# Two chunks' head products in one group, the bias product on two row tiles, and longer planned gaps in a gated state-space and expert layer

## The chip, the cores and the metric

The kernel runs on one core of a Trainium2 chip. The metric is the device time of one execution in microseconds (us). A core has a matrix engine (PE, with its weight loads shown apart as PEld), a vector engine (DVE), an activation engine (ACT), a general engine (POOL) and a queue that starts transfers (SP). Each executes its own instructions in order and waits on semaphores for the others. SBUF is the on-chip memory of 128 partitions; PSUM is the memory of eight banks of 128 x 512 fp32 that PE writes its products into.

## What is computed

The input is x, 8 sequences of 2048 tokens of 256 numbers. A modulation row per sequence gives shifts, scales and gates. The layer has two halves.

```
h = layernorm(x) * (1 + ca) + sa
x = x + ga * mamba(h)          # W_in, causal convolution, state space scan, gate by silu(z), RMS norm, W_out
h = layernorm(x) * (1 + cb) + sb
x = x + gb * experts(h)        # softmax gate over 8 experts, those under 0.1 dropped, sum of weight * (h @ W_e + b_e)
```

The scan is done by chunks. With C, B, the steps dt and the running sum cs of dt * A within a chunk, one of 8 heads of 64 channels gives

```
y[i] = sum over j <= i of (C_i . B_j) exp(cs_i - cs_j) dt_j x_j  +  exp(cs_i) C_i . state  +  D x_i
state' = exp(cs_last) state + sum over j of exp(cs_last - cs_j) dt_j B_j x_j
```

and y * silu(z) is squared and summed over 512 channels for the RMS norm. The reference uses chunks of 64 tokens; the kernel computes the same scan in chunks of 128.

## The kernel before, in words

The work is cut into 32 blocks of 512 tokens (8 sequences, 4 blocks each), and a block into four chunks of 128 tokens. Everything is fp32; a matrix product is issued by PE as two instructions, so the counts of the profile are twice those of the program. Weights stay in SBUF.

The steps of a block are generators. A planner (`run`) holds a heap of generators with due times; it takes the earliest, lets it write its next instructions, and puts it back later by what it yields. One planned block is `PERIOD` = 70. `STARTS` gives each step's first due time within its block, so that some four blocks are open at once: `fetch` (-20), `first_norm` (-9), `project_xbc` (11.5), `project_z` (42), `silu_xbc` (47.5), `output` (128), `gate_weights` (151) and `experts` (186); `within` starts for chunk c at 54 + 17.5 c. The planned clock decides only the order in which instructions are written, and with it the order on each engine of the built program; no engine waits for it.

PSUM is handed out by the planner too. `take(use)` gives the bank that has been free longest, at most `MOST[use]` to one use ("ex" expert products, "pj" projections, "y" heads, "m" the rest). `give` says that a bank is free again `READ_TIME` = 3.0 after the reader was written. The true protection is a semaphore: a product into a reused bank waits for the last reader.

The steps that the change touches:

- `spread` (L508) loads, for one chunk, the running sums cs of the 8 heads to all 128 partitions, into the first half of the tile `wide` (128 x 2 x 8 x 128).
- `within` (L517) makes the second half from it by eight Relu instructions on ACT (L526), then four transposes of x on PE (L536), that of B (L537) and the product B by C (L539); one Exp over both halves on ACT (L540); on DVE the scaled x, `xdt` (L543), the masked product (L547), B (L549) and the weights of the 8 heads, in place in `wide` (L561); on POOL `xdec` (L556) and `cw` (L564). Then come the products of the heads (L579): 8 of `xdt` by the weights and 8 of `state` by `cw`, each 64 columns wide, two heads side by side in the array; the state product (L587) with its decay on POOL (L590); on DVE the skip term (L600, four instructions), the gate by silu(z) (L603) and the new state (L609, or L607 at a start); at last the squares on ACT (L616) and their sums on POOL (L618, L619), into `sqs`.
- `output` (L626) transposes `sqs` (L633), which turns the squares by channel into rows by token, reduces them, and multiplies by W_out (L646); `residual` (L655) adds to x.
- `gate_weights` makes the second norm and the gate: a product (L673), a copy (L679), its transpose (L681), a softmax on DVE and ACT (L696), and the transposed weights `wtt` (L712, L715). `eb_sb` holds the experts' biases: rows 32 c to 32 c + 7 of column block c.
- `experts` (L739) starts `res` with the product of `wtt` and `eb_sb` (L748, two products of 128 x 512 with all 128 rows of the array, most of which are zeros) and an ACT copy (L753). Then follow 16 pairs of expert products (L759), each read by two DVE instructions (L722); POOL adds to x and SP stores the block.

Of the kernel before, what the change touches and what calls it, by code (L numbers as in the profile page):

```python
# [11 lines left out]
AF = mybir.ActivationFunctionType  # L12
# [3 lines left out]
P = 128  # L16
# [9 lines left out]
def kernel(  # L26
# [51 lines left out]
    const = ctx.enter_context(tc.tile_pool(name="const", bufs=1))  # L78
    psum = ctx.enter_context(tc.tile_pool(name="psum", bufs=1, space=bass.MemoryType.PSUM))
    N_BANKS = 8  # L80
    MOST = {"ex": 3, "pj": 2, "y": 1, "m": 4}


    ident = new(const, [P, P], "ident")
# [5 lines left out]
    neg_half = new(const, [P, NC], "neg_half")  # L90
    nc.gpsimd.memset(neg_half, -0.5)

    io = ctx.enter_context(tc.tile_pool(name="io", bufs=4))

    pb = ctx.enter_context(tc.tile_pool(name="per_batch", bufs=2))
    blk = ctx.enter_context(tc.tile_pool(name="block", bufs=2))
# [411 lines left out]
    def spread(n, c):  # L508

        yield from until(info[n], "cs_d")  # L510
        wide = info[n]["wide", c] = new(chk, [P, 2, NH, P], "wide")
        nc.sync.dma_start(
            out=wide[:, 0], in_=info[n]["cs_d"][c * QD : c * QD + NH, :].partition_broadcast(P)
        )
        yield

    def within(n, c):  # L517


        d = info[n]  # L520
        yield from until(d, "tok", ("wide", c))
        xbc, tok_major, wide = d["xbc"], d["tok"], d["wide", c]
        tok = ts(c, P)
        bt, ct_ = xbc[:, MB, tok], xbc[:, MCC, tok]
        for h in range(NH):
            nc.scalar.activation(  # L526
                wide[:, 1, h, :], wide[:, 0, h, :], AF.Relu, bias=tok_major[:, 1, c, h : h + 1]
            )
# [11 lines left out]
        nc.scalar.activation(wide, wide, AF.Exp, scale=-1.0)  # L540
        yield 1.2
        xdt = new(chk, [P, DI], "xdt")
# [17 lines left out]
        up_to, w = wide[:, 0], wide[:, 1]  # L560
        nc.vector.tensor_tensor(w, w, sm[:, None, :].to_broadcast([P, NH, P]), ALU.mult)  # L561
        yield 1.8
        cw = new(chk, [P, NH, P], "cw")
        nc.gpsimd.tensor_tensor(cw, up_to, ct_[:, None, :].to_broadcast([P, NH, P]), ALU.mult)  # L564
        yield 2.0
        if c > 0:
            yield from until(d, ("state", c - 1))
        elif s_of(n) > 0:
            yield from until(info[n - 1], ("state", NC - 1))
        yield 3.5  # L570
        state = carry.get("state") if (s_of(n), c) != (0, 0) else None


        y_ps = yield from take("y")
        parts = [(xdt, w)] if state is None else [(xdt, w), (state, cw)]
        for i, (lhs, rhs) in enumerate(parts):
            for h in range(NH):
                m, q = divmod(h, 2)
                nc.tensor.matmul(  # L579
                    y_ps[ts(q, HEADDIM), ts(m, P)], lhs[:, ts(h, HEADDIM)], rhs[:, h, :],  # L580
                    start=(i == 0 and m == 0), stop=(i == len(parts) - 1),
                    skip_group_check=True,
                )
        if not last:

            st_ps = yield from take("m")
            nc.tensor.matmul(st_ps[:, :DI], bm, xdec, start=True, stop=True)  # L587
            behind = new(blk, [P, DI], "state", bufs=3)
            if state is not None:
                nc.gpsimd.tensor_tensor(  # L590
                    by_head(behind), by_head(state), per_head(up_to[:, :, P - 1]), ALU.mult
                )
            carry["state"] = behind
        d["state", c] = True
        yield from until(d, *(("z_silu", m) for m in range(MI)))
        yield 1.4
        y = y_ps.rearrange("p (m t) -> p m t", m=MI)
        g = d["zs"]
        for m in range(MI):
            nc.vector.scalar_tensor_tensor(  # L600
                y[:, m, :], xbc[:, m, tok], d_ch[:, m : m + 1], y[:, m, :], ALU.mult, ALU.add
            )
        nc.vector.tensor_tensor(g[:, :, tok], y, g[:, :, tok], ALU.mult)  # L603
        give(y_ps)
# [6 lines left out]
        yield 1.8  # L611

        if c == 0:
            d["sqs"] = new(sml, [P, NC, P], "sqs", bufs=1)
        sq = new(chk, [P, MI, P], "sq", bufs=1)
        nc.scalar.activation(sq, g[:, :, tok], AF.Square)  # L616
        yield 0.8
        nc.gpsimd.tensor_add(sq[:, 0:2, :], sq[:, 0:2, :], sq[:, 2:4, :])  # L618
        nc.gpsimd.tensor_add(d["sqs"][:, c, :], sq[:, 0, :], sq[:, 1, :])  # L619
        d["y", c] = True  # L620

    def s_of(n):
        return order[n][1]
# [2 lines left out]
    def output(n):  # L626
        b, s = order[n]
        d = info[n]
        yield from until(d, *(("y", c) for c in range(NC)))
        wo = gated[b][0]  # L630
        s_ps = yield from take("m")
        for c in range(NC):
            nc.tensor.transpose(s_ps[:, ts(c, P)], d["sqs"][:, c, :], ident)  # L633
        yield 1.2
        ms = new(sml, [P, NC], "ms")
        nc.vector.tensor_reduce(ms, s_ps.rearrange("p (c t) -> p c t", c=NC), AX.X, ALU.add)
        give(s_ps)
        yield 0.9
        rs = new(sml, [P, NC], "rs")
        inv_sqrt(rs, ms, 1.0 / DI)  # L640
        yield 1.0
        d["mv"] = new(sml, [P, NC, 2], "mv1")
        for c in range(NC):
            o_ps = yield from take("m")
            for m in range(MI):
                nc.tensor.matmul(  # L646
                    o_ps[:, :DM], d["zs"][:, m, ts(c, P)], wo[:, m, :],
                    start=(m == 0), stop=(m == MI - 1),
                )
            after(2.2, residual(n, c, o_ps, rs))  # L650
            yield OUT_STEP
# [11 lines left out]
    def gate_weights(n):  # L663
# [13 lines left out]
        yield 1.2  # L677
        head = new(sml, [P, P], "head", bufs=1)
        nc.scalar.copy(head, lg_ps[:, :P])  # L679
        yield 1.5  # L680
        nc.tensor.transpose(lg_ps[:, P : 2 * P], head, ident)  # L681
        yield 1.0

# [22 lines left out]
        nc.vector.scalar_tensor_tensor(wsum, wsum, 0.0, wsum, ALU.is_equal, ALU.add)  # L706
        nc.vector.reciprocal(wsum, wsum)
        nc.vector.tensor_mul(w, w, over(wsum))
        yield 6.5

        wt_ps = yield from take("m")
        nc.tensor.transpose(wt_ps[:, :P], wt.rearrange("p c q -> p (c q)"), ident)  # L712
# [26 lines left out]
    def experts(n):  # L739
        d = info[n]  # L740
        yield from until(d, "wtt")
        ht, wtt = d["ht", 1], d["wtt"]
        per = 512 // DM

        res = new(blk, [P, NC, DM], "res")
        for c in range(0, NC, per):
            b_ps = yield from take("m")
            nc.tensor.matmul(  # L748
                b_ps, wtt, eb_sb[:, c : c + per, :].rearrange("p c o -> p (c o)"),
                start=True, stop=True,  # L750
            )
            yield 1.2
            nc.scalar.copy(res[:, c : c + per, :].rearrange("p c o -> p (c o)"), b_ps)  # L753
            give(b_ps)
        for c in range(NC):
            for e in range(0, NE, per):
                ps = yield from take("ex")
                for k in range(KD):
                    nc.tensor.matmul(  # L759
                        ps, ht[:, k, ts(c, P)],  # L760
                        we_sb[:, k, e : e + per, :].rearrange("p e o -> p (e o)"),
                        start=(k == 0), stop=(k == KD - 1),
                    )
# [58 lines left out]
```

## Time and profile before

| what | value |
| --- | --- |
| median of 3 runs | 2448.13 us (2447.92 to 2448.78) |
| the profiled execution, its own time | 2448.43 us |
| span of its profile | 2446.6 us |
| mean granted PE clock | 0.992 |
| busy DVE / ACT / POOL | 1850.2 / 1437.3 / 1094.1 us |
| instructions | 33352 |

The profile describes one execution. Busy time of an engine is the time in which it executes anything. The timeline gives start, duration, engine, line, operation and output<-inputs, with equal neighbours merged; since matrix products overlap at their ends, the distance from start to start tells what one costs. The table of waits says which instruction stood idle and what released it.

### The profile page before, as it was taken

The page shows a single profiled execution, that of the slowest core. Times are in us where ns is not written, and L with a number is a line of the kernel's source. Part 1 is how long each engine was busy: PE and PEld are TensorE (multiplying, and loading weights), DVE is VectorE, ACT ScalarE, POOL GpSimd, SP SyncE. Part 2 cuts the span into 40 slices and gives each one's busy share as a digit, 9 for nine tenths or more (in the row PEclk, how much of TensorE's full clock was granted, in tenths as well). Part 3 has the DMA queues.
Part 4 walks back from the last instruction along what each step waited for, and adds up shares of the span by engine and source line. Part 5 has one row for each costly group of instructions (what it writes and reads, how often), then busy time and mean ns, then how long its engine had stood idle before and what let it go on. Part 6 is the DMA issues. An engine that isn't in the chain of part 4 may idle for free.

```text
span 2446.6 us, 33352 instructions
## 1 busy us (share of the span) xinstructions
PE 2356.1 (96%) x11474; PEld 1312.8 (54%) x11474; DVE 1850.2 (76%) x4414; ACT 1437.3 (59%) x2685; POOL 1094.1 (45%) x1244
## 2 busy tenths in 40 slices
PE   7899999999999999999999999999999999999998
PEld 3555555555555555555555555555555555555554
DVE  5677877777777777877777877878777777778775
ACT  6776666566566556655665565665556656555630
POOL 3544444444444434444444444444445444454441
PEclk8899999999999999999999999999999999999999
DMA  5111111111111111011111011110111111111100
GB/s 153 37 36 45 41 40 45 53 45 45 39 42 45 52 45 45 31 49 45 44 46 53 28 45 48 49 45 28 50 46 45 45 37 44 45 44 54 36 27 18
DMA packets 64600, 110.49 MB, mean 45 GB/s; under 512 B 7048, under 2 KB 47024, under 8 KB 64432
## 3 DMA queue, kind: packets, MB, share of 16 engines
q1 hardware_dynamic: 64416, 108.35, 13.2%
q8 instruction: 92, 1.51, 0.3%
q14 instruction: 76, 0.62, 0.1%
q10 hardware_dynamic: 16, 0.01, 0.0%
HBM read 89.47 MB, written 18.87 MB: 44 GB/s over the span
## 4 chain that ended last, share of the span: by engine, by line
PE 37%; DVE 21%; ACT 20%; POOL 11%; DMA 7%; issue 3%; SPq 0%; ACTq 0%; POOLq 0%; DVEq 0%
PE bank L759 15%; DVE xbc L372 6%; PE bank L409 5%; PE bank L445 5%; POOL cw L564 5%; ACT wide L526 5%; ACT wide L540 5%; DMA wide<-cs_d 4%; PE bank L579 4%; DVE res L722 3%; ACT xn L328 3%; DVE bank L600 2%; PE bank L646 2%; DMA xt<-_attn_hidden_states_dram 2%; POOL rstd L311 2%
## 5 line engine op out<-in xcount | busy, mean ns | idle before, releaser
L759 PE MATMUL bank<-we_sb,ht 128*128 128x512 f32 x2048 | 976.3, 599 | 41.4 <-DVE zs L603 39.2
L759 PEld LDWEIGHTS bank<-we_sb,ht 128*128 128x128 f32 x2048 | 368.7, 191 | 390.6 <-issue 367.2
L722 DVE SCALAR_TENSOR_TENSOR res<-bank,wt,res 128x256 f32<-128x256 f32 x1024 | 485.3, 474 | 99.8 <-PE bank L759 65.6
L372 DVE SCALAR_TENSOR_TENSOR xbc<-bank,conv_w_sb,xbc 128x509 f32<-128x509 f32 (+2 forms) x576 | 426.3, 742 | 82.0 <-ACT halo L368 78.2
L526 ACT ACTIVATE wide<-wide,tok_major 128x128 f32<-128x128 f32 x1024 | 329.0, 388 | 199.4 <-DMA wide<-cs_d 141.1
L564 POOL TENSOR_TENSOR cw<-wide,xbc 128x1024 f32<-128x1024 f32 x128 | 315.6, 2466 | 186.4 <-ACT wide L540 133.9
L409 PE MATMUL bank<-ht,w_in_sb 128*128 128x512 f32 x768 | 365.3, 598 | 3.0 <-ACT ht L340 2.6
L590 POOL TENSOR_TENSOR state<-state,wide 128x512 f32<-128x512 f32 x112 | 118.6, 1059 | 285.4 <-DVE state L609 263.4
L540 ACT ACTIVATE wide<-wide 128x2048 f32<-128x2048 f32 x128 | 244.7, 1912 | 2.3
L328 ACT ACTIVATE xn<-xt,shift,rstd 128x256 f32<-128x256 f32 x256 | 135.4, 591 | 182.8 <-DVE shift L324 182.8
L646 PE MATMUL bank<-wo,zs 128*128 128x256 f32 x1024 | 242.7, 380 | 0.0
L600 DVE SCALAR_TENSOR_TENSOR bank<-xbc,d_ch,bank 128x128 f32<-128x128 f32 x512 | 179.5, 351 | 82.3 <-PE bank L579 75.6
L445 PE MATMUL bank<-ht,w_in_sb 128*128 128x512 f32 x512 | 240.9, 594 | 0.0
L618 POOL TENSOR_TENSOR sq<-sq 128x256 f32<-128x256 f32 x128 | 103.1, 805 | 287.0 <-ACT sq L616 282.8
L409 PEld LDWEIGHTS bank<-ht,w_in_sb 128*128 128x128 f32 x768 | 141.0, 192 | 160.7 <-issue 131.6
L646 PEld LDWEIGHTS bank<-wo,zs 128*128 128x128 f32 x1024 | 192.2, 190 | 64.8 <-issue 33.7
L730 POOL TENSOR_TENSOR res<-res,gates 128x256 f32<-128x256 f32 x128 | 93.5, 731 | 258.0 <-DVE res L722 258.0
L561 DVE TENSOR_TENSOR wide<-wide,sm 128x1024 f32<-128x1024 f32 x128 | 204.2, 1595 | 0.0
L556 POOL TENSOR_TENSOR xdec<-xdt,tok_major 128x512 f32<-128x512 f32 x120 | 132.9, 1108 | 126.1 <-DVE xdt L543 120.3
L364 ACT ACTIVATE xbc<-bank,conv_b_sb,conv_w_sb 128x512 f32<-128x512 f32 x192 | 147.2, 767 | 35.8 <-PE bank L409 35.6
L616 ACT ACTIVATE sq<-zs 128x512 f32<-128x512 f32 x128 | 79.8, 624 | 147.3 <-DVE zs L603 94.2
L445 PEld LDWEIGHTS bank<-ht,w_in_sb 128*128 128x128 f32 x512 | 96.3, 190 | 119.2 <-issue 106.5
(127 smaller groups left out, 3098.8 us busy)
## 6 DMA issues: line engine op xcount, KB each, us to landing
wide<-cs_d SPq DMA_DIRECT2D x128, 512.0 KB
xt<-_attn_hidden_states_dram SPq DMA_DIRECT2D x32, 512.0 KB
out_dram<-xt SPq DMA_DIRECT2D x32, 512.0 KB
we_sb<-in_L_ffn_expert_w_dram SPq DMA_DIRECT2D x8, 256.0 KB
cs_d<-cs SPq DMA_DIRECT2D x32, 64.0 KB
ht<-in_L_wmod_dram SPq DMA_DIRECT2D x2, 512.0 KB
w_in_sb<-in_L_attn_W_in_dram SPq DMA_DIRECT2D x1, 776.0 KB
w_in_sb<-in_L_attn_W_in_dram SPq DMA_DIRECT2D x1, 512.0 KB
```

Of the source, the lines that this page charges most:

```text
L328: nc.scalar.activation(xn[:, c, :], src[:, c, :], AF.Identity, bias=shift[:, c : c + 1], scale=rstd[:, c : c + 1],)
L372: nc.vector.scalar_tensor_tensor(acc[:, ahead:], ps[:, : T - ahead], conv_w_sb[:, m, k : k + 1], acc[:, ahead:], ALU.mult, ALU.add,)
L409: nc.tensor.matmul(ps, w_in_sb[:, k, DI + m * P : DI + (m + 1) * P], ht[:, k, :], start=(k == 0), stop=(k == KD - 1),)
L445: nc.tensor.matmul(ps, w_in_sb[:, k, ts(m, P)], ht[:, k, :], start=(k == 0), stop=(k == KD - 1),)
L526: nc.scalar.activation(wide[:, 1, h, :], wide[:, 0, h, :], AF.Relu, bias=tok_major[:, 1, c, h : h + 1])
L540: nc.scalar.activation(wide, wide, AF.Exp, scale=-1.0)
L561: nc.vector.tensor_tensor(w, w, sm[:, None, :].to_broadcast([P, NH, P]), ALU.mult)
L564: nc.gpsimd.tensor_tensor(cw, up_to, ct_[:, None, :].to_broadcast([P, NH, P]), ALU.mult)
L600: nc.vector.scalar_tensor_tensor(y[:, m, :], xbc[:, m, tok], d_ch[:, m : m + 1], y[:, m, :], ALU.mult, ALU.add)
L646: nc.tensor.matmul(o_ps[:, :DM], d["zs"][:, m, ts(c, P)], wo[:, m, :], start=(m == 0), stop=(m == MI - 1),)
L722: nc.vector.scalar_tensor_tensor(res, ps[:, ts(q, DM)], wt[:, c, e + q : e + q + 1], res, ALU.mult, ALU.add)
L759: nc.tensor.matmul(ps, ht[:, k, ts(c, P)], we_sb[:, k, e : e + per, :].rearrange("p e o -> p (e o)"), start=(k == 0), stop=(k == KD - 1),)
```

## The change

Heads. `wide` keeps only cs and its exponential; the weights get a tile `w` of their own with three buffers, `xdt` and `cw` get three and the state four. The one Exp over 2048 elements becomes two over 1024. `within` now writes the state product (now L576), its decay (L579) and the new state (L590) and stores the operands of the heads. After the second and the fourth chunk a new function, `outputs`, takes two banks and writes the head products of two chunks as one run of 32 (L608), then for each of the two the skip term (L620), the gate (L624), the squares (L631) and the sums (L633, L634).

Biases. The two products over 128 rows become four products of 64 rows and 256 columns (L768), in turns on the upper and the lower rows, into two banks that are taken together; the two copies (L774) follow.

Planned times. `READ_TIME` goes from 3.0 to 4.5, the yield before the gate's transpose (now L697) from 1.5 to 3.5, that before the transposed weights (L728) from 6.5 to 8.0; `output` yields 5.0 before the transposed squares (L649); `gate_weights` starts at 156 and `experts` at 198; the input tiles get five buffers, not four, and "y" two banks. The expert products are now L781 and their readers L738.

```diff
-    MOST = {"ex": 3, "pj": 2, "y": 1, "m": 4}
+    MOST = {"ex": 3, "pj": 2, "y": 2, "m": 4}
-    io = ctx.enter_context(tc.tile_pool(name="io", bufs=4))
+    io = ctx.enter_context(tc.tile_pool(name="io", bufs=5))
 def spread(n, c):
-        wide = info[n]["wide", c] = new(chk, [P, 2, NH, P], "wide")
+        wide = info[n]["wide", c] = new(chk, [P, NH, P], "wide")
 def within(n, c):
+        w = new(chk, [P, NH, P], "w", bufs=3)
         for h in range(NH):
             nc.scalar.activation(
-                wide[:, 1, h, :], wide[:, 0, h, :], AF.Relu, bias=tok_major[:, 1, c, h : h + 1]
+                w[:, h, :], wide[:, h, :], AF.Relu, bias=tok_major[:, 1, c, h : h + 1]
             )
...
         nc.scalar.activation(wide, wide, AF.Exp, scale=-1.0)
+        nc.scalar.activation(w, w, AF.Exp, scale=-1.0)
...
-        y_ps = yield from take("y")
-        parts = [(xdt, w)] if state is None else [(xdt, w), (state, cw)]
-        for i, (lhs, rhs) in enumerate(parts):
-            for h in range(NH):
...
         if not last:
             st_ps = yield from take("m")
             nc.tensor.matmul(st_ps[:, :DI], bm, xdec, start=True, stop=True)
-            behind = new(blk, [P, DI], "state", bufs=3)
+            behind = new(blk, [P, DI], "state", bufs=4)
...
         d["state", c] = True
+        d["parts", c] = [(xdt, w)] if state is None else [(xdt, w), (state, cw)]
+        yield 1.5
         if not last:
...
+        if c % 2:
+            yield 1.5
+            yield from outputs(n, c - 1)
+
+    def outputs(n, first):
+        d = info[n]
+        xbc, g = d["xbc"], d["zs"]
+        pair = yield from take("y", 2)
+        for j, y_ps in enumerate(pair):
+            parts = d["parts", first + j]
+            for i, (lhs, rhs) in enumerate(parts):
+                for h in range(NH):
+                    m, q = divmod(h, 2)
+                    nc.tensor.matmul(
+                        y_ps[ts(q, HEADDIM), ts(m, P)], lhs[:, ts(h, HEADDIM)], rhs[:, h, :],
+                        start=(i == 0 and m == 0), stop=(i == len(parts) - 1),
+                        skip_group_check=True,
+                    )
+        yield from until(d, *(("z_silu", m) for m in range(MI)))
+        for j, y_ps in enumerate(pair):
+            c = first + j
+            tok = ts(c, P)
+            yield 1.4
...
+            give(y_ps)
+            yield 1.8
...
+            nc.scalar.activation(sq, g[:, :, tok], AF.Square)
+            yield 0.8
...
 def output(n):
+        yield 5.0
         s_ps = yield from take("m")
 def gate_weights(n):
         nc.scalar.copy(head, lg_ps[:, :P])
-        yield 1.5
+        yield 3.5
...
-        yield 6.5
+        yield 8.0
 def experts(n):
-        for c in range(0, NC, per):
-            b_ps = yield from take("m")
-            nc.tensor.matmul(
-                b_ps, wtt, eb_sb[:, c : c + per, :].rearrange("p c o -> p (c o)"),
-                start=True, stop=True,
-            )
-            yield 1.2
-            nc.scalar.copy(res[:, c : c + per, :].rearrange("p c o -> p (c o)"), b_ps)
+        half = P // 2
+        pair = yield from take("m", 2)
+        for j in range(2):
+            for q, b_ps in enumerate(pair):
+                rows = ts(q, half)
+                nc.tensor.matmul(
+                    b_ps[:, ts(j, DM)], wtt[rows, :], eb_sb[rows, 2 * q + j, :],
+                    start=True, stop=True,
+                )
+        yield 1.2
+        for q, b_ps in enumerate(pair):
+            nc.scalar.copy(res[:, 2 * q : 2 * q + 2, :].rearrange("p c o -> p (c o)"), b_ps)
             give(b_ps)
+            yield 0.6
-    READ_TIME = 3.0
+    READ_TIME = 4.5
-        (silu_xbc, 47.5), (output, 128.0), (gate_weights, 151.0), (experts, 186.0),
+        (silu_xbc, 47.5), (output, 128.0), (gate_weights, 156.0), (experts, 198.0),
```

More of the change, by code (lines that the diff above doesn't have):

```diff
@@ L510, in spread @@
         yield from until(info[n], "cs_d")
-        wide = info[n]["wide", c] = new(chk, [P, 2, NH, P], "wide")
+        wide = info[n]["wide", c] = new(chk, [P, NH, P], "wide")
         nc.sync.dma_start(
-            out=wide[:, 0], in_=info[n]["cs_d"][c * QD : c * QD + NH, :].partition_broadcast(P)
+            out=wide, in_=info[n]["cs_d"][c * QD : c * QD + NH, :].partition_broadcast(P)
         )
@@ L540, in within @@
         nc.scalar.activation(wide, wide, AF.Exp, scale=-1.0)
+        nc.scalar.activation(w, w, AF.Exp, scale=-1.0)
         yield 1.2
-        xdt = new(chk, [P, DI], "xdt")
+        xdt = new(chk, [P, DI], "xdt", bufs=3)
         nc.vector.tensor_tensor(
@@ L559, in within @@
         yield 0.6
-        up_to, w = wide[:, 0], wide[:, 1]
         nc.vector.tensor_tensor(w, w, sm[:, None, :].to_broadcast([P, NH, P]), ALU.mult)
         yield 1.8
-        cw = new(chk, [P, NH, P], "cw")
-        nc.gpsimd.tensor_tensor(cw, up_to, ct_[:, None, :].to_broadcast([P, NH, P]), ALU.mult)
+        cw = new(chk, [P, NH, P], "cw", bufs=3)
+        nc.gpsimd.tensor_tensor(cw, wide, ct_[:, None, :].to_broadcast([P, NH, P]), ALU.mult)
         yield 2.0
@@ L571, in within @@
         state = carry.get("state") if (s_of(n), c) != (0, 0) else None
-        y_ps = yield from take("y")
-        parts = [(xdt, w)] if state is None else [(xdt, w), (state, cw)]
-        for i, (lhs, rhs) in enumerate(parts):
-            for h in range(NH):
[L578 to L582, printed above, removed]
-                )
         if not last:
@@ L587, in within @@
             nc.tensor.matmul(st_ps[:, :DI], bm, xdec, start=True, stop=True)
-            behind = new(blk, [P, DI], "state", bufs=3)
+            behind = new(blk, [P, DI], "state", bufs=4)
             if state is not None:
                 nc.gpsimd.tensor_tensor(
-                    by_head(behind), by_head(state), per_head(up_to[:, :, P - 1]), ALU.mult
+                    by_head(behind), by_head(state), per_head(wide[:, :, P - 1]), ALU.mult
                 )
@@ L594, in within @@
         d["state", c] = True
[L595 to L604, printed above, removed]
+        d["parts", c] = [(xdt, w)] if state is None else [(xdt, w), (state, cw)]
+        yield 1.5
         if not last:
@@ L610, in within @@
             give(st_ps)
[L611 to L620, printed above, removed]
+        if c % 2:
[20 more added lines that the diff above has]
+            yield 1.4
+            y = y_ps.rearrange("p (m t) -> p m t", m=MI)
+            for m in range(MI):
+                nc.vector.scalar_tensor_tensor(
+                    y[:, m, :], xbc[:, m, tok], d_ch[:, m : m + 1], y[:, m, :],
+                    ALU.mult, ALU.add,
+                )
+            nc.vector.tensor_tensor(g[:, :, tok], y, g[:, :, tok], ALU.mult)
+            give(y_ps)
+            yield 1.8
+            if c == 0:
+                d["sqs"] = new(sml, [P, NC, P], "sqs", bufs=1)
+            sq = new(chk, [P, MI, P], "sq", bufs=1)
+            nc.scalar.activation(sq, g[:, :, tok], AF.Square)
+            yield 0.8
+            nc.gpsimd.tensor_add(sq[:, 0:2, :], sq[:, 0:2, :], sq[:, 2:4, :])
+            nc.gpsimd.tensor_add(d["sqs"][:, c, :], sq[:, 0, :], sq[:, 1, :])
+            d["y", c] = True
     def s_of(n):
@@ L745, in experts @@
         res = new(blk, [P, NC, DM], "res")
-        for c in range(0, NC, per):
-            b_ps = yield from take("m")
-            nc.tensor.matmul(
-                b_ps, wtt, eb_sb[:, c : c + per, :].rearrange("p c o -> p (c o)"),
-                start=True, stop=True,
-            )
-            yield 1.2
-            nc.scalar.copy(res[:, c : c + per, :].rearrange("p c o -> p (c o)"), b_ps)
+        half = P // 2
[6 more added lines that the diff above has]
+                    start=True, stop=True,
+                )
+        yield 1.2
+        for q, b_ps in enumerate(pair):
+            nc.scalar.copy(res[:, 2 * q : 2 * q + 2, :].rearrange("p c o -> p (c o)"), b_ps)
             give(b_ps)
+            yield 0.6
         for c in range(NC):
```

## The prediction

> **What bounds the kernel now.** I read the busy times first, then PE's waits, then its timeline for the price of single steps.
>
> ```profile
> PE 2356.1 (96%) x11474; PEld 1312.8 (54%) x11474; DVE 1850.2 (76%) x4414; ACT 1437.3 (59%) x2685; POOL 1094.1 (45%) x1244
> ```
>
> PE is busy 96%, the next engine 76%. The table of stretches (columns: stretch, length, then busy time of PE, PEld, DVE, ACT, POOL, at the end PE's clock, DMA share and GB/s) tells where the rest is.
>
> ```profile
> 0.00:160.00 160.00, 127.38 (x630) 73.12 (x631) 104.74 (x249) 118.89 (x209) 68.67 (x89) 0.91 0.27 83
> ...
> 310.00:2360.00 2050.00, 2002.84 (x9840) 1118.14 (x9840) 1581.23 (x3777) 1218.99 (x2288) 938.49 (x1054) 1.00 0.13 43
> ```
>
> From 310 on PE is busy 97.7% at full clock: only fewer PE microseconds or fewer PE stalls shorten that stretch. PE's waits after 160 us:
>
> ```profile
> PE bank L759 <- DVE zs L603: 39.2, 20, 2.4
> PE bank L681 <- ACT head L679: 5.5, 6, 1.2
> PE bank L409 <- ACT ht L340: 1.9, 2, 1.0
> ```
>
> The table's seven rows sum to 50.6 us; one line holds 39.2. Now PE's timeline around a group of heads and a bias product:
>
> ```profile
> 1207.38 1.88 PE L759 MATMUL bank<-we_sb,ht 128*128 128x512 f32 x4
> 1209.19 1.09 PE L579 MATMUL bank<-wide,xdt 128*64 128x128 f32 x16
> 1210.21 1.13 PE L587 MATMUL bank<-xdec,bm 128*128 128x512 f32 x2
> 1211.18 1.89 PE L646 MATMUL bank<-wo,zs 128*128 128x256 f32 x8
> ...
> 1259.77 1.88 PE L748 MATMUL bank<-eb_sb,wtt 128*128 128x512 f32 x4
> 1261.49 1.02 PE L759 MATMUL bank<-we_sb,ht 128*128 128x512 f32 x2
> 1262.34 1.88 PE L445 MATMUL bank<-ht,w_in_sb 128*128 128x512 f32 x4
> 1264.15 1.09 PE L579 MATMUL bank<-wide,xdt 128*64 128x128 f32 x16
> 1265.08 1.04 PE L579 MATMUL bank<-cw,state 128*64 128x128 f32 x16
> 1266.05 1.12 PE L587 MATMUL bank<-xdec,bm 128*128 128x512 f32 x2
> 1267.01 1.88 PE L445 MATMUL bank<-ht,w_in_sb 128*128 128x512 f32 x4
> ```
>
> Start to start, four 128x512 take 1.72 us (1259.77 to 1261.49), so 0.43 each. From 1207.38 to 1211.18 are 3.80; less six of 0.43 (2.58) the 16 head products cost 1.22. From 1262.34 to 1267.01 are 4.67; less 2.58 the 32 cost 2.09. So 16 more cost 0.87, and the visit itself 1.22 - 0.87 = 0.35: about 0.09 late on entry (1209.19 is 1.81 after 1207.38), the remainder in the filling and the exit. The price of 0.87 is half of 16 times 0.107, so two heads do run side by side.
>
> The main stall, as PE shows it:
>
> ```profile
> 1308.66 1.52 PE L759 MATMUL bank<-we_sb,ht 128*128 128x512 f32 x3 [2.16 <-DVE zs L603]
> ```
>
> This expert product takes over the bank of the heads' products of one chunk. DVE's timeline ends that gate (L603) at 1308.52; four L600 and L603 stood between the instructions of the step size chain (L471 to L487), which waits for an ACT table. The planner had counted 3.0 for it.
>
> **What the Trainium skill says.** "TensorEngine Tiling (Array Packing)", section "Key Properties": a change of the tiling mode drains the array. The 0.35 us per visit agrees. "TensorE: Matmul & The Clock Gate", section "Part 3: Packing small matmuls": products on different row or column tiles run together, four row tiles at 3.07 times the speed. The columns' side agrees (0.87); no run here shows row tiles. The tiling page, "Restrictions and Gotchas": row tiles must write different banks; the change gives them two. "ScalarE: Activation LUTs", section "What ACT_TABLE_LOAD costs": a switch of function sets costs a load of 1283 ns and a drain of 1380. The trace has the load at exactly 1283 ns and no drain: the next ACTIVATE starts as the load ends.
>
> ```profile
> L540 ACT ACT_TABLE_LOAD x37 | 47.5, 1283 | 0.7
> L432 ACT ACT_TABLE_LOAD x35 | 44.9, 1283 | 0.6
> ```
>
> **The change part by part.** The sum is made against the profiled execution, 2448.4 us (span 2446.6 and 1.8 outside); the median of the runs, 2448.1, is the same within 0.3.
>
> *Heads in pairs.* The streaming work stays. In the issue order of the two built programs, runs of heads' products fall from 131 to 69 (three and five of the groups are cut by other products): 62 x 0.35 = 21.7 saved. Part is given back: 22 of the old runs lay against a 32-wide product (L459, L673), only 7 of the new. Sharing a visit saves 0.20 (1223.31 to 1228.55 in the timeline holds six full products, 16 of L459 and 32 heads: 5.24 - 2.58 = 2.66; apart they cost 0.77 and 2.09). 15 x 0.20 = 3.0. Net -18.7. All of it is on PE, which sets the end.
>
> *Bias.* Now 32 x 1.72. After: eight instructions of 256 columns on two row tiles stream what 16 of 128 columns do, 0.87, and make a visit, 0.35: 1.22. Saved 32 x 0.50 = 16.0. Bounds: a visit that costs nothing saves 32 x 0.85 = 27; tiles that run one after the other cost 1.72 + 0.35 and lose 32 x 0.35 = 11. I take 16, because the column tiles behave so. The two ACT copies remain.
>
> *Stalls.* With `READ_TIME` 4.5 no bank of the heads is taken over again, from the fourth block on, before 6.16 us of PE work (the products in between at the prices above); before it was 4.94 at 19 places, which are the stalls of 2.4. DVE freed that bank about 7.4 us after its last product in the worst chunk. Hence that stall shrinks to some 1 us or nothing. The gate's transpose gets 2.0 more planned time against stalls of at most 1.2: 5.5 goes. What is late next: the banks of the chunks' transposes (x, and B with its product), which DVE reads at L543 to L549. Their shortest distance falls from 6.02 to 3.76, at 18 places under 5, while DVE sometimes ends bm (L549) 7 us after the product began, in the chunk behind the step size chain. Following the new DVE order by hand at the old durations, that chunk's bm ends about 14.3 us after L459 starts, with PE due there at 14.6: a close call. The banks of z and bias are taken over after 4.96 (9 places) and 4.74 (13). I count 50.6 as gone and 20 as new (bounds 5 and 55): -31.
>
> *ACT.* Two Exps of 1024 for one of 2048: 1059 ns (L427's row of 128x1024) twice less 1912 ns is +0.2, x128 = 26 us. More important: in the built order the Exps alternate with the Silus of z and xbc, and the table loads go from 155 to 289: 134 x 1.283 = 172 us. ACT goes from 1437 to about 1635 us, 69% of the new span. I charge nothing beyond the 20 of new stalls: ACT runs ahead (it waits 182.8 us for the second norm's shift, 141.1 for `wide` to arrive), and PE waited after 160 us only 7.4 for ACT. If that cover is gone a load costs PE up to 1.28.
>
> *Moved steps.* The state product leaves its place behind the heads; it needs only bm and xdec, and PE waits 5.8 for it in all, within the first 120 us. Its DVE addition now stands ahead of the heads' skip terms, so POOL's decay and `cw` come no later. `output` is some 8 planned us later, gate 5, experts 12; with the experts POOL's two instructions and the store on SP. On SP the next x load stands behind that store; the fifth buffer is for this. `wide` is no longer held by the weights, so its load is issued earlier. None lies on PE's path: 0. The first bias product has 95.3 us of PE work ahead of it before and 94.7 after, the last is 27.5 and 27.7 from the end: start and tail stay, +-8.
>
> Sum: 2448.4 - 18.7 - 16.0 - 31 = 2382.7, said as 2383.
>
> **The rivals.** *Row tiles do not overlap* (the bias part does not do what it says): 2383 + 16 + 11 = 2410. For: no row tile in the trace; against: the same array overlaps columns. *The stall only moves*, to the transposes' banks: all 50.6 come back but for the 20 counted, 2383 + 31 = 2414. For: 3.76 against 6.02; against: those readers are mostly quicker, median 3.2 us for bm. *Slower: ACT's loads reach PE.* Between z, xbc and Exp a load stands in ACT's queue ahead of the Silu that frees a projection's bank, and of the Silu of xbc that the transposes wait for. Gains are 66 us, so from 66 / 1.283 = 51 of the 134 loads on PE's path the change loses; with two thirds of them, 89 x 1.283 = 114, it is 2383 + 114 = 2497. For: the loads cluster in that phase, two or three within one chunk; against: 69% busy, and PE's few waits for ACT. *All goes well*: no visit cost for the bias and 5 us of stalls: 2383 - 11 - 15 = 2357.
>
> **How the numbers follow.** Likeliest 0.62 (own range 2363 to 2403), all well 0.09, row tiles 0.06, moved stalls 0.12, slower by ACT 0.08, and near no change from several of these together 0.03. About 0.2% (5 us) is what a measurement can tell from no change. So faster 0.89, same 0.03, slower 0.08. The range, 2352 to 2422, takes in the first four and leaves out the last two.
>
> **What would show it.** Right: heads' runs of 64 instructions (3.84 us start to start by 0.35 + 4 x 0.87), bias near 1.2 us with its products starting in pairs, PE's wait for the gate (L624) under 10 us, ACT table loads 289 and ACT near 1635 us. Wrong: bias near 2 us; a wait of L781 for bm (L551) or for Silu (L432) above 20 us; or a busy PE share below 95% after 310 us.

## The result, and the profile after

The changed kernel takes 2407.5 us (median of 4, 2407.1 to 2408.3), the kernel before in the same comparison 2448.3 (2447.9 to 2448.8). The ratio is 0.9834, with a 95% interval of 0.9817 to 0.9851: 41 us faster, where 65 were forecast. It lies in the range of 2352 to 2422. The profiled execution took 2408.3 us, with a span of 2406.5 and a mean clock of 0.988.

The same views as before, of the kernel after. First the busy times, and from the table of stretches the line of 310 to 2360 us:

```profile
PE 2327.3 (97%) x11602; PEld 1313.9 (55%) x11602; DVE 1830.3 (76%) x4414; ACT 1621.4 (67%) x2947; POOL 1128.7 (47%) x1244
```

```profile
310.00:2360.00 2050.00, 2018.19 (x10137) 1145.28 (x10136) 1586.71 (x3837) 1389.94 (x2528) 981.92 (x1073) 1.00 0.13 44
```

PE is still the bound: 98.4% busy from 310 on (97.7% before), and ACT has grown by 184 us. The timeline of PE has a group of heads and a bias product close together:

```profile
1113.35 1.88 PE L781 MATMUL bank<-we_sb,ht 128*128 128x512 f32 x4
1115.16 1.09 PE L608 MATMUL bank<-w,xdt 128*64 128x128 f32 x16
1116.08 1.04 PE L608 MATMUL bank<-cw,state 128*64 128x128 f32 x16
1116.95 1.04 PE L608 MATMUL bank<-w,xdt 128*64 128x128 f32 x16
1117.83 1.04 PE L608 MATMUL bank<-cw,state 128*64 128x128 f32 x16
1118.80 0.33 PE L728 MATMUL bank<-ident,wt 128*128 128x128 f32 x1
1118.97 1.88 PE L445 MATMUL bank<-ht,w_in_sb 128*128 128x512 f32 x4
1120.69 1.88 PE L781 MATMUL bank<-we_sb,ht 128*128 128x512 f32 x4
1122.50 1.13 PE L768 MATMUL bank<-eb_sb,wtt 64*128 64x256 f32 x8
1123.56 1.98 PE L445 MATMUL bank<-ht,w_in_sb 128*128 128x512 f32 x4
```

The steps between the four lines of L608 are 0.92, 0.87 and 0.88: the stream of 16 costs what it did, and there is one entry and one exit for 64. Taken against their neighbours' undisturbed distances, 54 clean runs of 64 have a median of 3.84 us. From 1120.69 to 1123.56 are 2.87; less four products of 0.43 (1.72) that leaves 1.15, and the product behind is 0.10 longer than usual (1.98 against 1.88); from start to start over several products the bias costs 1.26 instead of 1.72. So the row tiles do run side by side.

PE's waits after 160 us (what stood idle, what released it: sum, times, longest):

```profile
PE bank L781 <- DVE bm L551: 15.6, 8, 3.1
PE bank L576 <- POOL xdec L558: 6.4, 13, 0.8
PE bank L649 <- POOL sqs L634: 5.1, 4, 1.7
```

The old wait for the gate (39.2 us) is gone, and so is that for the head (5.5). All rows together are 38.2 us, against 50.6. What is late now is B's copy, in the bank that an expert product takes over. The timeline of all engines ahead of the first of its four stalls of 3.1 us:

```profile
703.70 0.99 ACT L527 ACTIVATE w<-wide,tok_major 128x128 f32<-128x128 f32 x3 [2.33 <-PE bank L608]
...
709.73 0.62 ACT L631 ACTIVATE sq<-zs 128x512 f32<-128x512 f32 x1
...
710.43 0.72 POOL L633 TENSOR_TENSOR sq<-sq 128x256 f32<-128x256 f32 x1 [6.20 <-ACT sq L631]
...
711.92 1.02 POOL L311 TENSOR_TENSOR rstd<-rstd,neg_half 128x4 f32<-128x4 f32 x1
...
712.91 2.34 POOL L565 TENSOR_TENSOR cw<-wide,xbc 128x1024 f32<-128x1024 f32 x1
712.97 2.30 DVE L324 SCALAR_TENSOR_TENSOR shift<-mv,rstd 128x4 f32<-128x4 f32 x1 [3.87 <-POOL rstd L311]
...
715.20 0.68 DVE L624 TENSOR_TENSOR zs<-bank,zs 128x512 f32<-128x512 f32 x1
...
717.25 0.28 DVE L551 COPY bm<-bank 128x128 f32<-128x128 f32 x1
...
717.58 3.56 PE L781 MATMUL bank<-we_sb,ht 128*128 128x512 f32 x4 [3.15 <-DVE bm L551]
```

Read it from the bottom. PE waits for the copy of B. It stands in DVE's queue behind the gate (L624) and the first norm's shift (L324), which waits 3.87 for POOL's root. POOL had stood 6.20 at the head of its queue, waiting for a Square; the Square stood in ACT's queue behind norm copies and Relus, and began two microseconds after its input was there (707.80). The first of these Relus (703.70) had stood 2.33 for PE, which was still reading the buffer of `w` from the pair before (L608), and from there to the Square ACT had no pause. All four stalls of 3.1 us have such a Relu ahead of them, each with 2.3 us. Three queues in order, each late by what stood ahead, and the wait at the new tile `w` is where it begins. The second field of L781 shows a further price: its four products take 3.56 instead of 1.88.

To account for the 40.3 us between the first and the last product of the two traces: PE's instructions and visits, summed at their undisturbed prices, fall from 2298.6 to 2265.4, -33.2 (bias -14.6, heads -18.6). Waits after 160 us give -12.4, those before 160 us +0.9, and products at half rate +4.4 (20 products of 128x512 that took 0.80 us or more with no wait, 9.1 us too long in all; before 11, 4.7 us). The sum is -40.3. The shorter stream came in full. The stalls did not.

### The profile page after: what moved, and what is told of

Its sections match the earlier page's. It is cut to its first block, busy times and chain, and to the rows that moved or that the text cites. A ratio compares the mean times of both kernels' runs of the same rounds, so it can differ in the third digit from the quotient of the medians.

```text
span 2406.5 us, 33568 instructions
## 1 busy us (share of the span) xinstructions
PE 2327.3 (97%) x11602; PEld 1313.9 (55%) x11602; DVE 1830.3 (76%) x4414; ACT 1621.4 (67%) x2947; POOL 1128.7 (47%) x1244
## 4 chain that ended last, share of the span: by engine, by line
PE 61%; ACT 11%; DVE 7%; POOL 6%; issue 1%; POOLq 0%; ACTq 0%
PE bank L781 26%; PE bank L662 8%; PE bank L409 7%; PE bank L445 6%; PE bank L608 4%; PE bank L576 3%; ACT w L527 3%; DVE xbc L372 2%; POOL cw L565 2%; PE bank L338 1%; PE bank L537 1%; ACT xn L328 1%; POOL rstd L311 1%; ACT wide L541 1%; DVE res L738 1%
## 5 line engine op out<-in xcount | busy, mean ns | idle before, releaser
L781 PE MATMUL bank<-we_sb,ht 128*128 128x512 f32 x2048 | 968.7, 598 | 18.3 <-DVE bm L551 15.6
L738 DVE SCALAR_TENSOR_TENSOR res<-bank,wt,res 128x256 f32<-128x256 f32 x1024 | 487.3, 476 | 212.6 <-PE bank L781 116.5
L781 PEld LDWEIGHTS bank<-we_sb,ht 128*128 128x128 f32 x2048 | 375.5, 191 | 398.8 <-issue 351.8
L372 DVE SCALAR_TENSOR_TENSOR xbc<-bank,conv_w_sb,xbc 128x511 f32<-128x511 f32 (+2 forms) x576 | 425.4, 740 | 96.0 <-ACT halo L368 94.9
L565 POOL TENSOR_TENSOR cw<-wide,xbc 128x1024 f32<-128x1024 f32 x128 | 305.7, 2388 | 274.5 <-ACT wide L541 157.2
L527 ACT ACTIVATE w<-wide,tok_major 128x128 f32<-128x128 f32 x1024 | 327.2, 390 | 137.8 <-PE bank L608 96.2
L409 PE MATMUL bank<-ht,w_in_sb 128*128 128x512 f32 x768 | 375.1, 611 | 5.6 <-DVE xbc L372 4.5
L445 PE MATMUL bank<-ht,w_in_sb 128*128 128x512 f32 x512 | 244.6, 601 | 1.0 <-ACT zs L432 1.0
L579 POOL TENSOR_TENSOR state<-state,wide 128x512 f32<-128x512 f32 x112 | 120.8, 1079 | 247.1 <-DVE state L590 216.7
L340 ACT ACTIVATE ht<-bank,mod_pp 128x512 f32<-128x512 f32 x128 | 97.7, 776 | 188.9 <-PE bank L338 188.8
L746 POOL TENSOR_TENSOR res<-res,gates 128x256 f32<-128x256 f32 x128 | 133.4, 1042 | 149.2 <-DVE res L738 142.4
L620 DVE SCALAR_TENSOR_TENSOR bank<-xbc,d_ch,bank 128x128 f32<-128x128 f32 x512 | 176.6, 349 | 20.7 <-PE bank L608 11.8
L562 DVE TENSOR_TENSOR w<-w,sm 128x1024 f32<-128x1024 f32 x128 | 189.0, 1477 | 0.0
L633 POOL TENSOR_TENSOR sq<-sq 128x256 f32<-128x256 f32 x128 | 99.2, 775 | 124.4 <-ACT sq L631 124.2
L576 PE MATMUL bank<-xdec,bm 128*128 128x512 f32 x240 | 130.1, 625 | 12.7 <-POOL xdec L558 6.4
```

The source lines that it names most:

```text
L372: nc.vector.scalar_tensor_tensor(acc[:, ahead:], ps[:, : T - ahead], conv_w_sb[:, m, k : k + 1], acc[:, ahead:], ALU.mult, ALU.add,)
L409: nc.tensor.matmul(ps, w_in_sb[:, k, DI + m * P : DI + (m + 1) * P], ht[:, k, :], start=(k == 0), stop=(k == KD - 1),)
L445: nc.tensor.matmul(ps, w_in_sb[:, k, ts(m, P)], ht[:, k, :], start=(k == 0), stop=(k == KD - 1),)
L527: nc.scalar.activation(w[:, h, :], wide[:, h, :], AF.Relu, bias=tok_major[:, 1, c, h : h + 1])
L565: nc.gpsimd.tensor_tensor(cw, wide, ct_[:, None, :].to_broadcast([P, NH, P]), ALU.mult)
L620: nc.vector.scalar_tensor_tensor(y[:, m, :], xbc[:, m, tok], d_ch[:, m : m + 1], y[:, m, :], ALU.mult, ALU.add,)
```

## The experiments

A table first. "waits" is the sum of PE's waits after 160 us, "half" the time lost to products at half rate after 160 us, "loads" the count of ACT's table loads. The ratio is to the kernel before, run beside it, with its 95% interval.

| kernel | us | ratio | waits | half | loads |
| --- | --- | --- | --- | --- | --- |
| before | 2448.3 | 1 | 50.6 | 4.7 | 155 |
| after | 2407.5 | 0.9834 (0.9817 to 0.9851) | 38.2 | 9.1 | 289 |
| before, biases on row tiles | 2451.1 | 1.0007 (0.9999 to 1.0016) | 63.1 | 6.3 | 155 |
| pairs alone | 2565.7 | 1.0480 (1.0462 to 1.0497) | 128.0 | 19.5 | 221 |
| pairs and two gaps | 2483.6 | 1.0152 (1.0135 to 1.0169) | 78.0 | 11.5 | 227 |
| before with the gaps | 2392.0 | 0.9765 (0.9751 to 0.9780) | 2.0 | 0.0 | 235 |
| the same with the biases | 2388.3 | 0.9756 (0.9741 to 0.9770) | 8.8 | 0.0 | 235 |
| after, one tile, one Exp | 2370.1 | 0.9675 (0.9660 to 0.9689) | 11.9 | 4.4 | 243 |
| the same, old biases | 2383.5 | 0.9738 (0.9724 to 0.9753) | 12.9 | 1.4 | 251 |
| after, one tile, two Exps | 2375.5 | 0.9703 (0.9688 to 0.9717) | 16.9 | 2.3 | 259 |
| after, one tile of two buffers | 2440.7 | 0.9966 (0.9953 to 0.9978) | 59.7 | 7.2 | 261 |
| after, three buffers of `wide` | 2409.5 | 0.9841 (0.9825 to 0.9858) | 40.7 | 8.1 | 287 |
| after, four buffers of `w` | 2492.0 | 1.0180 (1.0165 to 1.0196) | 94.5 | 23.0 | 257 |
| after, squares' sums later | 2398.4 | 0.9798 (0.9783 to 0.9812) | 30.4 | 4.0 | 285 |

**The parts alone.** The kernel before with the biases on row tiles, and nothing else:

```diff
 def experts(n):
-            b_ps = yield from take("m")
-            nc.tensor.matmul(
-                b_ps, wtt, eb_sb[:, c : c + per, :].rearrange("p c o -> p (c o)"),
...
+        pair = yield from take("m", 2)
...
+                nc.tensor.matmul(
+                    b_ps[:, ts(j, DM)], wtt[rows, :], eb_sb[rows, 2 * q + j, :],
...
```

> The kernel before with the biases alone on two row tiles; nothing else moves. The product's price in the changed kernel's trace is 1.26 us against 1.72, so 32 x 0.46 = 14.6 saved. Theory that PE's streaming time is the bound and stalls stay as they are: 2434 (2430 to 2438), PE's wait for the gate (L603) still near 39 us. Rival, that the stalls take up what PE saves (DVE is no quicker, so a shorter way to the bank means a longer wait): 2443 or more, and the wait grows by 9 us or more.

Measured: no gain, 1.0007. PE's waits:

```profile
PE bank L764 <- DVE zs L603: 44.9, 26, 2.4
PE bank L409 <- ACT ht L340: 6.8, 7, 1.0
```

The wait for the gate grew from 39.2 to 44.9, that for the copies of `ht` from 1.9 to 6.8; all rows from 50.6 to 63.1. That is 12.5 of the 14.6 us that the stream lost. A PE that is quicker only comes sooner here to a bank that DVE frees at its own time.

The changed kernel with all gaps and the biases as they were before, so that the pairs, the tile `w` and the two Exps remain (called "pairs alone" below):

```diff
-    READ_TIME = 4.5
+    READ_TIME = 3.0
...
-        (silu_xbc, 47.5), (output, 128.0), (gate_weights, 156.0), (experts, 198.0),
+        (silu_xbc, 47.5), (output, 128.0), (gate_weights, 151.0), (experts, 186.0),
...
-    io = ctx.enter_context(tc.tile_pool(name="io", bufs=5))
+    io = ctx.enter_context(tc.tile_pool(name="io", bufs=4))
...
         wo = gated[b][0]
-        yield 5.0
...
         nc.scalar.copy(head, lg_ps[:, :P])
-        yield 3.5
+        yield 1.5
...
-        yield 8.0
+        yield 6.5
```

> The changed kernel with the old planned gaps (READ_TIME 3.0, the old yields and starts, four input buffers) and the old bias product; only the pairs of heads, with the separate weights tile and two Exps, remain. 62 fewer visits give -18.7 in streaming. Theory that the pairs by themselves do not take the stalls away and only the gaps do: 2425 to 2440, PE's waits after 160 us 40 us or more. Rival, that the later place of the heads' group is what ends the old stall, with no need of the gaps: 2395 to 2412, waits under 25 us.

Measured: 2565.7, 116 us slower than before, far from either. Its two largest waits, behind two of the removed yields:

```profile
PE bank L648 <- POOL sqs L634: 97.0, 50, 3.8
PE bank L696 <- ACT head L694: 25.4, 26, 3.0
```

The kernel before with the gaps alone (the lines above, the other way round):

> The kernel before with the planned gaps alone (READ_TIME 4.5, the longer yields, the later starts, five input buffers). No streaming time is saved. Theory that the gaps take the stalls of before (50.6 us after 160 us and about 20 at half clock behind them): 2400 to 2425, waits after 160 us under 25 us, although the built order has 235 table loads instead of 155. Rival, that the 80 more loads on ACT eat it: 2440 or more.

Measured: 2392.0, which is 57.6 faster than before and 15.5 faster than the whole change. Nothing of its heads or biases differs from before. The first row of PE's waits, and PE from 310 on:

```profile
PE bank L579 <- DVE wide L561: 0.9, 3, 0.3
```

```profile
310.00:2360.00 2050.00, 2046.35 (x10035) 1140.67 (x10036) 1625.10 (x3852) 1313.51 (x2370) 1003.19 (x1068) 1.00 0.13 44
```

This is the largest of three rows, which sum to 2.0 us, and PE is busy 99.8%. No product at half rate is left after 160 us; before there were 4.7 us of it, not the 20 that were expected. The wider gaps are thus the best part of the change by itself, and ACT's 80 more table loads do no harm there.

**The weights' tile.** The changed kernel, with cs and the weights in one tile again, as before, but with three buffers, and one Exp:

```diff
-        wide = info[n]["wide", c] = new(chk, [P, NH, P], "wide")
+        wide = info[n]["wide", c] = new(chk, [P, 2, NH, P], "wide", bufs=3)
...
-        w = new(chk, [P, NH, P], "w", bufs=3)
+        wide, w = both[:, 0], both[:, 1]
...
-        nc.scalar.activation(wide, wide, AF.Exp, scale=-1.0)
-        nc.scalar.activation(w, w, AF.Exp, scale=-1.0)
+        nc.scalar.activation(both, both, AF.Exp, scale=-1.0)
```

> The changed kernel with weights and decay in one tile of three buffers again and one Exp of 2048 elements; table loads in the built order fall from 289 to 243, and ACT saves 46 x 1.28 + 26 = 85 us of busy time. Theory that ACT's loads are not on PE's path (the missing 24 us are PE's waits for a DVE that stands behind POOL): within 6 us of the changed kernel, 2401 to 2413. Rival, that the loads are what keeps the gain at 41 us: each load on the path gives back up to 1.28, so 2395 or less (half of 46 on the path are 29 us).

Measured: 2370.1, the fastest of all, 37 below the change and 79 below the kernel before. Two things differ, ACT's work and the buffers. The next four were to tell them apart. One more buffer for the weights, the rest as changed:

```diff
-        w = new(chk, [P, NH, P], "w", bufs=3)
+        w = new(chk, [P, NH, P], "w", bufs=4)
```

> The changed kernel with a fourth buffer for the heads' weights w, nothing else. New theory after the run with one Exp: a pair of heads keeps two weights buffers until PE has run it, so with three ACT stands at the next chunk's Relus until PE's heads are done (ACT waits 90 us on L608 between 310 and 2300), and all that is behind it on ACT, squares, convolution, bias copies, comes late. Then a fourth buffer takes that wait away at the same number of table loads (about 289): 2370 to 2390. Rival, that the table loads do it: the loads stay, so 2402 to 2412.

Measured: 2492.0, slower than before. ACT's waits after 160 us:

```profile
ACT w L527 <- DMA wide<-cs_d: 275.3, 41, 11.8
```

With a buffer at hand the Relus no longer wait for PE; they stand at the head of ACT's queue for the transfer of `wide` instead, up to 11.8 us each, and the copies that PE needs stand behind them (PE's largest wait is for `ht`, 55.5 us). Neither expectation held, and the fourth buffer did more than lift a wait. The plan is the same, yet the table loads, expected to stay at 289, fell to 257: the two traces show ACT's instructions in another order, with the Relus of 82 of the 128 chunks earlier in ACT's queue (by up to 11 instructions) and none later. So the order on an engine isn't the planner's alone; the build (the step that turns the written instructions into each engine's program) moves it with the number of buffers, and a run that changes a buffer count changes both. The one tile with one Exp, but two buffers:

```diff
-        wide = info[n]["wide", c] = new(chk, [P, 2, NH, P], "wide", bufs=3)
+        wide = info[n]["wide", c] = new(chk, [P, 2, NH, P], "wide")
```

> The changed kernel with one Exp and one tile for both halves, but two buffers of it, not three; table loads in the built order 261 against 289 (changed) and 243 (one Exp, three buffers). Table loads as the cause: between the two, 2375 to 2395, nearer 2385. Buffers as the cause: with two buffers a pair holds both, the next chunk can't begin, so far worse than the changed kernel: 2430 or more.

Measured: 2440.7, and PE waits 49.6 us for the squares' sums. So the one Exp isn't enough. (Here nearly every chunk's Relus stand later in ACT's queue than with three buffers, by 9 instructions in the mean.) A third buffer for `wide` in the changed kernel, with `w` apart:

```diff
-        wide = info[n]["wide", c] = new(chk, [P, NH, P], "wide")
+        wide = info[n]["wide", c] = new(chk, [P, NH, P], "wide", bufs=3)
```

> The changed kernel with a third buffer for wide alone (the sums and their exponentials); w keeps three. Loads 287. If the weights' buffer is what holds ACT: no change, 2400 to 2412. If it was the third wide buffer that made the run with one Exp fast (an earlier transfer): 2365 to 2380.

Measured: 2409.5, as the change itself. A third buffer of cs isn't enough either. Last, the one tile of three buffers with two Exps on its halves, which has the buffers of the fast kernel (and as many as the one just told) and most of ACT's work of the change:

```diff
-        nc.scalar.activation(both, both, AF.Exp, scale=-1.0)
+        nc.scalar.activation(wide, wide, AF.Exp, scale=-1.0)
+        nc.scalar.activation(w, w, AF.Exp, scale=-1.0)
```

> The kernel with one tile of three buffers for both operands of the Exp (2370), with two Exps of 1024 columns on its halves instead of one of 2048. The buffers and the transfer's conditions stay; ACT gets 128 Exps more, and table loads go from 243 to 259 (16 x 1.28 = 21 us), together some 47 us of ACT's time. Theory A (what the one Exp brought was ACT's time: fewer instructions and loads): 2395 to 2410. Theory B (what it brought was that both operands share their buffers, so that no Relu takes a buffer that PE still reads): 2370 to 2376.

Measured: 2375.5, theory B. ACT is busy 33 us more than with one Exp, for 5 us of time. The kernel with three buffers of `wide` and three of `w` has ACT busy another 38 us, at 2409.5: at that exchange, which is an estimate, ACT's work explains 6 of the 34 us between the two. PE's order is the same in both but for 8 of 11602 products, and PE's waits and half rate together are 48.8 us with `w` apart and 19.2 with one tile. What is left is where the buffer is waited for, together with the order on ACT that the build makes of it: with one tile the Relus of 72 of the 128 chunks stand a few instructions later in ACT's queue, and none earlier. ACT's largest row for the Relus (L527) in the kernel with `w` apart, from 310 to 2300 us:

```profile
ACT w L527 <- PE bank L608: 89.3, 41, 2.8
```

and all its rows for them in the one-tile kernel with two Exps:

```profile
ACT wide L527 <- DVE tok_major L502: 38.8, 19, 3.6
...
ACT wide L527 <- DMA wide<-cs_d: 22.2, 20, 3.0
```

With `w` apart, ACT stands 89 us for PE to read the weights of the pair before, with the Squares and copies behind it in its queue. In the changed kernel itself it is 90.2 us, 42 times. With one tile that row is gone, and the wait for PE belongs to the transfer (SP, L512; the same stretch), which has no such row with `w` apart. PE's wait for B's copy, 15.8 us with `w` apart and three buffers of `wide`, shrinks as well:

```profile
SPq L512 <- PE bank L608: 1330.1, 86, 36.7
```

```profile
PE bank L781 <- DVE bm L551: 2.1, 4, 0.5
```

So the shared tile is worth 34 us. How much of that is the place of the wait and how much the later place of the Relus in ACT's queue, these runs do not part. Four buffers of `w` with three of `wide` were not tried.

**The chain through the squares.** The changed kernel, with POOL's sums as a step of their own, planned 4.0 behind the Square (0.8 before), and two buffers for the squares:

```diff
-            sq = new(chk, [P, MI, P], "sq", bufs=1)
+            sq = new(chk, [P, MI, P], "sq", bufs=2)
             nc.scalar.activation(sq, g[:, :, tok], AF.Square)
+            after(4.0, sums(d, c, sq))
             yield 0.8
-            nc.gpsimd.tensor_add(sq[:, 0:2, :], sq[:, 0:2, :], sq[:, 2:4, :])
-            nc.gpsimd.tensor_add(d["sqs"][:, c, :], sq[:, 0, :], sq[:, 1, :])
-            d["y", c] = True
...
+    def sums(d, c, sq):
...
```

> The changed kernel, with the two sums of squares on POOL written as a step of their own, planned 4.0 us behind the Square on ACT instead of 0.8, with two buffers for the squares. Theory (long stalls begin when POOL stands at the head of its queue before these sums, up to 6 us, with the root of the norm, the shift, B's copy and the experts' bank behind it): PE's waits for the copy of B (15.6 us in the changed kernel) fall under 5, POOL's wait for the Square falls, and the time is 2385 to 2395. Rival (POOL's wait is only one of several that can come last; ACT's Relus and Exps are late anyway): 2400 to 2410, with the waits moved to other banks.

Measured: 2398.4, between the two. The waits for B's copy fell from 15.6 in the bank of the experts to one of 2.7 in another. A new one came, for the transposed weights (`wtt`):

```profile
PE bank L772 <- ACT wtt L735: 12.9, 12, 1.6
...
PE bank L576 <- DVE bm L551: 2.7, 1, 2.7
```

So POOL's place in the chain read in the timeline is real: when it no longer stands there, these stalls go. The run is 9 us faster, but that isn't the price of the chain alone, since this edit also changes the order of PE's own products in more than half of their places; and another reader is then the last.

**Which gap the pairs lacked.** Pairs alone, with two yields put back, 5.0 ahead of the transposed squares and 3.5 ahead of the head's transpose:

```diff
         wo = gated[b][0]
+        yield 5.0
...
         nc.scalar.copy(head, lg_ps[:, :P])
-        yield 1.5
+        yield 3.5
```

> The run with pairs alone (2565.7), with two of the change's wider gaps put back: 5.0 us ahead of the transposed squares and 3.5 ahead of the head's transpose. The reading distance (3.0), the starts, the experts' delay, four input buffers and the old biases stay. Theory (pairs make the sums of squares of both chunks come late together, and the missing 5.0 is what made PE stand for them 50 times, 97 us, and for the head 26 times, 25 us): 2430 to 2450. Rival (every reader that the planner puts 3.0 behind its producer is too early once ACT and POOL carry more, so the other waits grow in their place): over 2500.

Measured: 2483.6, which is 82 us less than pairs alone. Neither theory gave that. The head's wait is gone, but the squares' sums still cost 34.5 us and the decayed x (`xdec`, on POOL) 29.3. Between pairs alone and the changed kernel lie 158 us: the two yields bring 82 of them, and the reading distance, the starts, the third yield, the fifth buffer and the biases, which were not parted further, bring the other 76.

**What a shorter stream is worth.** The row-tile biases (the first diff above) upon the kernel with the gaps:

> The kernel before with the planned gaps and the biases on two row tiles, heads one chunk at a time. With the gaps alone PE hardly waits after 160 us (2 us) and a block takes 72.65 us of PE's time. If a saving in PE's stream counts in full once the stalls are gone: 32 x 0.46 = 14.6 less than the 2392 of the gaps alone, so 2377 (2372 to 2383). Rival, that the stalls come back as they did with the bias product alone (which gained nothing): 2388 or more.

Measured: 2388.3, 3.7 less, which is hardly more than the scatter (2385.2 to 2391.1 here, 2390.6 to 2393.8 with the gaps alone). Counted from one block's product of the step sizes to the next, the late blocks (12 to 28) last 72.2 us instead of 72.7, which is the whole 0.46 of a block, but blocks 4 to 12 are 0.4 longer. New waits of 7.2 us stand ahead of a transpose (L497), and those before 160 us grow by 3.3. And from the fastest kernel the row tiles taken away (the first diff, the other way round):

> The kernel with one Exp a chunk (2370), with the biases as they were before: one product of 128 rows and 512 columns per bank. The bias products themselves are then 1.72 instead of 1.26 us a block, 14.6 us over 32 blocks. Theory (a shorter stream counts in full where PE's blocks already last as long as its stream): 2385, within 3. Rival (saved stream is taken up by waits here too, as it was when the biases alone were changed in the kernel before): 2370 to 2374. Rival 2 (the order that the planner builds moves with every edit and its effect is larger than the saving): anywhere over 2390 or under 2370.

Measured: 2383.5, 13.4 more, the theory (14.6). The same edit is thus worth nothing in the kernel before, where PE's waits grow by 12.5 us with it; 3.7 upon the gaps, where they start at 2.0 but grow by some 10; and 13.4 where they hardly move (12.9 without it, 11.9 with it). Few waits beforehand are not enough: what counts is that the edit makes no new ones.

## Why the prediction was right or wrong

The time lies within the stated range, but outside the likeliest case's own, 2363 to 2403; the rivals' cases hold it. Three terms came nearly as said, and one was mis-sized by 24 us.

*Heads in pairs, -18.7.* Right: runs of 64 at 3.84 us as said, and 18.6 in all.

*Bias, -16.0.* The mechanism is right; 1.26 us for 1.22, so -14.6.

*Stalls, -31.* This is the step that failed. Its first half held: the 50.6 us of old waits were to go, the gate's 39.2 and the head's 5.5 did, and the gaps alone show it (2.0 left). The gain was even under-priced, since with the waits the half-rate products go as well (4.7 us). The second half, "20 as new", was 38.2 of waits and 9.1 of half rate. The place was named, the close call at bm with 14.3 against 14.6. In the block shown above bm ended 20.1 us after L459 began, with PE due at 17.0; it missed by 3.1 us in four blocks. The call was worked out at the old durations and in DVE's order alone, while what was late came into DVE from ACT by way of POOL. Waits and half rate together gave 7.1 us (0.9 of new waits in the start included), not 31: 24 of the 24.8 us by which the forecast was low.

*ACT, 0.* Counts and busy time came as said (289 loads, 1621 us for 1635). (One reading was wrong: the 182.8 us that ACT waits for "the second norm's shift" are those of both norms, since L324 runs twice a block.) The rival that the loads reach PE isn't borne out: the time doesn't follow their number (235 loads at 2392.0, 257 at 2492.0, 259 at 2375.5). But "I charge nothing" was wrong for another reason, which stands under *Moved steps*: "`wide` is no longer held by the weights, so its load is issued earlier. None lies on PE's path: 0." The weights' own tile moved the wait for PE's reading from the transfer's queue to the head of ACT's. To put it back brought 34 us with two Exps against the kernel with as many buffers, the changed place of the Relus in ACT's order included. I had looked at what the split sets free and not at who now waits for it.

*Rivals.* "The stall only moves" has the mechanism nearest to what came, though not its path. Row tiles that don't overlap, and a slower kernel, did not come; the slower side was near all the same, since pairs without the gaps are 116 us slower.

What stays open: the edits also change the order that the planner writes or that the build makes of it, so no experiment moved one wait alone. From the kernel with gaps and biases to the kernel with one tile and one Exp the pairs bring 18.2 us by the medians and 14.2 by the profiled executions, against 18.6 of stream, although waits and half rate are 7.5 us higher there; 3 to 7 us of that sum are not explained.

## What to carry to other kernels

A saving on the engine that sets the end was paid here only as far as that engine's waits did not grow with it: widen the distances first (57.6 us by constants alone), then shorten the stream, and measure each on top of the other. When a tile is split or a step is grouped, ask which engine now waits for its buffer, and what stands behind that wait in its queue: here it was better to let a transfer wait there than an engine that serves three others. And look at the order on each engine before a number of buffers is called a cause, since it can move with that number.

## What the runs showed of the hardware

The 128x4 shift on DVE (L324) took 2.30 us at 712.97, for which the median is 0.16. The rows of that line in the trace (minimum, median and longest, in ns):

```profile
L324 DVE SCALAR_TENSOR_TENSOR shift<-mv,rstd x64: 134/163/2303, 11.8 to 2354.6; 128x4 f32<-128x4 f32 x64
```

Five of its 64 are this long, and each began 0.06 us after POOL's product `cw` (128x1024, 2.34 us) and ended with it; four of them stand ahead of the four stalls of 3.1 us. What else was held takes two inputs from SBUF too: the weights' product of L562 took 2.13 us where it began under `cw` (median of eight) and 1.50 elsewhere. Operations on PSUM did not mind (L620 takes 356 ns under `cw` and 350 without), nor the statistics of L315 with one input from SBUF (428 and 418). The Trainium skill, "SBUF — State Buffer", section "Terms", has this: DVE and GpSimd share a pair of ports that one of them locks for a whole instruction. The trace agrees for the five shifts, and gives a price: 2.30 less 0.16 are 2.1 us, by an estimate, out of a stall of 3.1.

After a stall PE may run at half rate. Of the four stalls of 3.1 us three are followed by three to five products of 128x512 at 0.85 us or more instead of 0.43, the one at 793.86 by none; the granted clock is 0.50 from 868 to 874 us and 1.00 from 793 to 798. "TensorE: Matmul & The Clock Gate", section "What's actually happening", puts the fall to half clock after an idle window of about 3.4 us that runs freely. That some equal stalls have it and one has not agrees; but here 3.15 us of standing were enough, and at 164.18 two stalls of 1.62 and 1.67 within 4 us, so for the length the measurement decides.
